# Edge masks in the degree stage, chunk 0 counted before h is split, 33 dense chunks: one change to a graph layer with a mixture of experts

## The chip, the cores and the metric

The kernel runs on one core of a Trainium2 chip. The metric is the time of one execution on the device in microseconds; for the kernel before, three runs gave 1665.93, 1668.72 and 1669.80, median 1668.72. All times inside an execution are read from the trace of one profiled execution, in microseconds from the start of its span. The engines are PE (matrix multiply), DVE (VectorE), ACT (ScalarE), POOL (GpSimd) and SP, which here only issues transfers.

## The reference

A graph of 6250 nodes with 256 features and 200,000 edges (`src`, `dst`, sorted by `dst`). Cut to what matters:

```
deg_out = clip(segment_sum(1, src), 1);  deg_in = clip(segment_sum(1, dst), 1)
h  = x * rsqrt(deg_out)[:, None]
m  = segment_sum(h[src], dst) * rsqrt(deg_in)[:, None]
u  = m @ W_gc + b_gc + (x @ W_res + b_res)
u2 = u + moe(u)           # softmax over the top 2 of 64 experts, 1024 slots each,
                          # expert: gelu(a @ w1 + b1) @ w2 + b2, 256 -> 512 -> 256
out = layernorm(x + batchnorm(u2) * gamma + beta)
```

`batchnorm` takes mean and variance over the nodes, `layernorm` over the features.

## The kernel before, in words

Edges are laid out in groups of 128, one group to a column of the edge tiles: 1563 groups that hold edges, in 1568 columns. Nodes are laid out in 50 tiles of 125.

*Degree stage (L445 to L489).* 49 turns take 32 columns each. In a turn DVE makes two one-hot tiles (`hot_row` and `hot_col`, recorded at L250), PE multiplies them into `degp` (L469), which so counts the out-degree of all nodes, and `project` (L425) multiplies one node tile by W_gc and W_res. The product with W_gc goes to `hrow` and becomes h; because the scaling by the degree is a factor for each row, W_gc is applied before the segment sum. From turn 8 on POOL and PE find, chunk by chunk, how many nodes lie below a place (`ind` L461, `held` L463), and `placed` turns that into offsets. ACT writes `mis` (L490 and the list `off`), the position of each edge's target inside its window of 128 nodes; POOL loads `dstf`, the targets as numbers.

*Seam (L493 to L573).* The degrees are folded into `pd`, clipped, and become `s_out` = 1/sqrt(degree). `dmax`, transposed by PE into `pdm`, tells whether every degree is small enough for an exact count (`okd`, `okc`). DVE computes the edge masks: `kd` is the place of the target inside its short range, `fit` whether it lies within the range the plan allows. The masks end in `key` (chunks), `keyg` (gathered groups), `mf` (the list of edges that fit nowhere, written to DRAM) and `nmis`, from which `redo` and `some` tell a loop at the end whether any edge is left over. Mixed with these lines, `halves(t0)` (L513) scales ten node tiles of h and splits each into two numbers of the matmul's reduced fp32 type, a high half by ACT (L517) and a rest by DVE (L520) or by ACT and POOL (L524, L525), and SP writes both to `h_dram`.

*Dense stage (from L580).* The plan (L76) cuts the edges, which grow sparser with the target's number, into two sorts. The first 1025 groups are 31 *chunks*: for each chunk PE counts, with one-hot tiles `lo` (L250) and `hotk` (L650), how many edges go from every node to every one of the 128 targets of the window (`pc`, L663), ACT adds the counts to the cleared tile `counts[c % 2]` (L674), and 50 multiplies (L681, L682: one for each half of h) turn counts times h into the sums. The counts of chunk c + 1 are issued among the multiplies of chunk c. A `spread` (L698) adds a chunk's sums at their rows. The other 538 groups are *gathered*, in 32 windows: POOL fetches 128 rows of h by an indirect DMA (L596) into a ring of 8 tiles, and PE multiplies by a one-hot of the targets (L601, L602). The code emits all this by hand in one order: the list `work` carries an estimate for each piece, and a gathered group is set in when the estimates add up to `LEAD` plus n times `every`. Steps for finished nodes (x pairs, L715 to L751: two node tiles of u, their logits and top two) run in the same stage; what is not finished by its end, 4 tiles here, is left over to the routing.

*Routing (from L940).* `going` (L973) are tiles of ones with a zero first column, the multiplier of a scan (L1027) that finds each token's rank within its expert; POOL sets them. `upto_b`, `ex` and the picks on DVE come before the scan. Then the experts and the final norms follow.

The order of each engine's instructions is the order in which the code emits them; engines wait for one another only by data and by buffers.

## Time and profile before

| what | us |
|---|---|
| median of three runs (lowest, highest) | 1668.72 (1665.93, 1669.80) |
| profiled execution, its time | 1663.35 |
| its span | 1661.2 |
| last turn of the degree stage ends, degrees read (L494) | 176.3 |
| first count of chunk 0 (L663) | 222.55 |
| first multiply of chunk 0 (L681) | 235.86 |
| first fetch of gathered rows (L596) | 238.06 |
| first and last spread (L698) | 276.2, 998.6 |
| busy: PE, DVE, ACT, POOL (share of the span) | 86%, 57%, 43%, 56% |

Times of day such as 176.3 are starts within the span. A busy PE is not PE at its peak, because matmuls are pipelined: two matmuls in a row may each be shown with 0.28 us though they start 0.12 us apart. The spacing of starts is what they cost. Busy shares over the whole span mix stages with different limits, so windows of one stage are what is to be read.

### The profile page before, as it was taken

To read this page: it belongs to the slowest core of one execution; us is meant where nothing else is said; L and a number is where in the kernel's file an instruction comes from. 1 tells how busy PE (TensorE), PEld (TensorE's weight loads), DVE (VectorE), ACT (ScalarE), POOL (GpSimd) and SP (SyncE) were. 2 spreads that over 40 slices of the span, in tenths; PEclk is the share of its full clock that TensorE was granted. 3 is DMA by queue.
4 is the path that set the end of the run, shared out by engine and by line. 5 is a ranking of instruction groups with operands and counts; after the bars stand their busy time and mean duration, and the time that the engine had idled before them with its cause. 6 is when DMAs were issued, how large, how long until landed. Compare 5 with 4: busy or idle time off the path is not lost. (4 is left out here: it accounts for less than half of the span.)

```text
span 1661.2 us, 30987 instructions
## 1 busy us (share of the span) xinstructions
PE 1430.9 (86%) x10301; PEld 1196.1 (72%) x10301; DVE 940.0 (57%) x1786; ACT 709.9 (43%) x1706; POOL 935.3 (56%) x992
## 2 busy tenths in 40 slices
PE   4999349889999999999999995499999999997920
PEld 2555137778898999999899993378788887875610
DVE  8999876567656566555555537823232232221896
ACT  2343584334565656555555531322222222222258
POOL 3242337777777777777777752056566666652000
PEclk8999759999999999999999996789999999999965
DMA  5899776777887788787878866469788898774924
GB/s 157 230 270 274 239 232 196 202 219 208 237 237 209 219 246 252 209 240 220 230 227 235 232 187 146 131 181 280 218 266 274 258 263 259 222 234 149 250 64 123
DMA packets 221098, 362.14 MB, mean 218 GB/s; under 512 B 24819, under 2 KB 149613, under 8 KB 220929
## 3 DMA queue, kind: packets, MB, share of 16 engines
q1 hardware_dynamic: 158039, 180.12, 37.6%
q0 software_dynamic: 55328, 172.48, 35.5%
q10 hardware_dynamic: 7562, 7.47, 1.6%
q8 instruction: 84, 1.38, 0.3%
q14 instruction: 85, 0.70, 0.1%
HBM read 279.11 MB, written 74.47 MB: 213 GB/s over the span
## 5 line engine op out<-in xcount | busy, mean ns | idle before, releaser
L596 POOL DMA_INDIRECT r<-h_dram,srcg x538 | 579.9, 1078 | 184.4 <-issue 67.4
L681 PE MATMUL sm<-hrow,counts 125*128 125x258 f32 x1550 | 498.8, 338 | 2.6 <-DMA h_dram<-hrow 2.6
L674 ACT CAST counts<-pc 128x300 f32 (+7 forms) x804 | 356.3, 443 | 238.3 <-PE pc L663 203.7
L682 PE MATMUL sm<-hrow,counts 125*128 125x256 f32 x1550 | 412.4, 282 | 0.0
L681 PEld LDWEIGHTS sm<-hrow,counts 125*128 125x128 f32 x1550 | 301.2, 194 | 7.3 <-ACT counts L674 2.8
L650 DVE TENSOR_TENSOR hotk<-key,iota_h 128x1400 bf16<-128x1400 f16 (+5 forms) x199 | 190.3, 958 | 200.0 <-PE pc L663 198.9
L663 PE MATMUL pc<-hotk,lo 128*128 128x300 bf16 (+7 forms) x1025 | 278.3, 306 | 23.9 <-DMA h_dram<-hrow 18.0
L682 PEld LDWEIGHTS sm<-hrow,counts 125*128 125x128 f32 x1550 | 296.1, 191 | 0.9
L1342 ACT ACTIVATE hT<-ph,b1c 128x128 f32<-128x128 f32 (+8 forms) x256 | 112.2, 439 | 331.0 <-PE ph L1340 318.9
L1352 PE MATMUL py<-w2s,hT 128*128 128x256 f32 (+3 forms) x992 | 237.8, 383 | 0.0
L1340 PE MATMUL ph<-xgT,w1s 128*128 128x128 f32 (+8 forms) x1024 | 209.3, 348 | 0.8 <-DVE xgT L1330 0.8
L601 PE MATMUL pg<-r,hot 128*128 128x258 f32 x538 | 177.2, 329 | 25.2 <-DMA r<-h_dram,srcg 24.0
L1352 PEld LDWEIGHTS py<-w2s,hT 128*128 128x128 f32 (+3 forms) x992 | 165.6, 175 | 39.4 <-DVE ys L1355 2.7
L1340 PEld LDWEIGHTS ph<-xgT,w1s 128*128 128x128 f32 x1024 | 169.8, 191 | 33.1 <-issue 13.0
L1306 POOL DMA_INDIRECT y_dram<-ys,dest x124 | 120.2, 969 | 107.8 <-DVE ys L1355 47.3
L1306 POOL DMA_INDIRECT xg<-x_dram,ids x124 | 120.2, 970 | 100.7 <-DVE ids L1257 60.6
L1355 DVE TENSOR_TENSOR ys<-py,b2s 128x256 f32<-128x256 f32 (+3 forms) x124 | 52.3, 422 | 188.6 <-PE py L1352 173.3
L602 PE MATMUL pg<-r,hot 128*128 128x256 f32 x538 | 151.2, 281 | 0.0
L663 PEld LDWEIGHTS <-lo 128*128 128x128 bf16 x1025 | 88.3, 101 | 61.9 <-issue 23.1
L601 PEld LDWEIGHTS pg<-r,hot 128*128 128x128 f32 x538 | 102.8, 191 | 39.6 <-DMA r<-h_dram,srcg 35.6
L832 DVE TENSOR_TENSOR hot<-keyg,iota_f 128x512 fp32r<-128x512 f16 (+3 forms) x146 | 94.4, 648 | 45.7 <-PE pg L602 45.5
L250 DVE TENSOR_TENSOR lo<-lo_b,iota 128x1024 bf16<-128x1024 bf16 x129 | 88.6, 688 | 48.7 <-PE pc L663 48.0
(328 smaller groups left out, 1748.2 us busy)
## 6 DMA issues: line engine op xcount, KB each, us to landing
w1s<-in_L_gnn_w_dram SPq DMA_DIRECT2D x64, 512.0 KB
w2s<-in_L_gnn_w_dram SPq DMA_DIRECT2D x64, 512.0 KB
y_dram<-zeros SPq DMA_DIRECT2D x48, 256.0 KB
yr<-y_dram SPq DMA_DIRECT2D x25, 448.0 KB
r<-h_dram,srcg POOLq DMA_INDIRECT x538, 4.2
b2s<-in_L_gnn_b_dram SPq DMA_DIRECT2D x64, 128.0 KB
h_dram<-hrow SPq DMA_DIRECT2D x5, 1344.0 KB
z_dram<-zeros ACTq DMA_DIRECT2D x7, 903.0 KB
```

The costliest lines, as they stand in the source:

```text
L596: G.indirect_dma_start(out=f32(r[:, :2 * D]), out_offset=None, in_=h_dram[:, :], in_offset=bass.IndirectOffsetOnAxis(ap=idx, axis=0))
L601: T.matmul(pg, hot, r[:, D:], start=first, stop=False)
L602: T.matmul(pg[:, :D], hot, r[:, :D], start=False, stop=last)
L650: V.tensor_tensor(hot, pairs(key, e, n, m), iota_h[:, None, :m, :].to_broadcast([128, n // 2, m, 2]), ALU.is_equal)
L663: T.matmul(pc, los[g // PAIRS][:, r // 2, :, r % 2], hots.pop(g), start=(i == 0), stop=(i == k - 1))
L674: S.copy(counts[c % 2][:, :, ds(live["at"][j % 8], w)], pc.rearrange("p (t w) -> p t w", w=w))
L681: T.matmul(sm, by, hrow[:, t, D:], start=(t == 0), stop=False)
L682: T.matmul(sm[:, :D], by, hrow[:, t, :D], start=False, stop=(t == NT - 1))
L1306: w = G.indirect_dma_start(**kw)
L1340: T.matmul(ph[:, :m], w1s[:, kk, c * 128:(c + 1) * 128], xgT[:, kk, :m], start=(kk == 0), stop=(kk == 1))
L1342: S.activation(hT[:, c, :m], ph[:, :m], AF.Gelu, bias=b1_e[:, c:c + 1])
L1352: T.matmul(py[:n], hT[:, c, k * 128:k * 128 + n], w2s[:, c, :], start=(c == 0), stop=(c == 3))
```

## The change

1. *Masks.* The masks are computed inside the turns of the degree stage, one operation in each of a list of turns (`masks`). `wide` holds the width less one; `kc` is `kd` clamped to the allowed range, `unfit` where that changes it, and the key is `kd` where it fits and far off where not, plus the width times `hi`, which eleven ACT activations make of `wide` in turn 2. `keyg` is written by ACT directly, for gathered groups alone. The sums for `nmis` come out of two ACT passes; `mf` is added and written by POOL in turns 43 and 44. `ind` starts at turn 9 (`FIRST_IND`), `placed` comes two turns later than before with the two added chunks. `away` has a third row, which DVE makes in `placed`.
2. *Seam.* The square root's table is loaded in turn 48; the last two projections come behind the square root and the reciprocal, and `pdm` behind them.
3. *Clears.* Both tiles of counts are cleared at the start: the first in five pieces by DVE, POOL, DVE, POOL, ACT, the second in five by POOL. `counts[1]` is no longer cleared by ACT between the counts of chunk 0.
4. *Halves.* `halves(t)` handles one pair of tiles: two ACT activations and two DVE operations, nothing on POOL. Two pairs stand at the first `hotk` tiles, ten between the counts of chunk 0 (one for every fourth count), thirteen between its multiplies (t = 0, 2, ... 24). The first eight fetches and the first one-hots of gathered rows (`first_rows`) are issued behind the last pair. `left_edges` (the left-over check) stands at t = 45 of chunk 0.
5. *Plan.* 33 chunks with 1061 groups, 502 gathered groups in 30 windows, `LEAD` 76. Six node tiles are left over to the routing.
6. *Routing.* ACT fills `going`.

```diff
-LEAD = 30.0
+LEAD = 76.0
...
-    while 16.0 + 1.03 * (pe + (NGU - g) * 0.265) < (NGU - g) * 1.29:
+    while 16.0 + 1.03 * (pe + (NGU - g) * 0.265) < (NGU - g) * 1.42:
...
+            masks = {
+                8: lambda: V.tensor_tensor(kd, dstf[:, :GD], base, ALU.subtract),
+                11: lambda: V.scalar_tensor_tensor(kc, kd, 0.0, upmost, op0=ALU.max, op1=ALU.min),
+                14: lambda: V.tensor_tensor(unfit, kc, kd, ALU.not_equal),
+                17: lambda: V.scalar_tensor_tensor(kd, unfit, -4096.0, kc, op0=ALU.mult, op1=ALU.add),
+                20: lambda: V.tensor_tensor(key[:, :GD], kd, wide, ALU.add),
+                22: lambda: S.activation(kd, unfit, AF.Copy, accum_out=nmis[:, 0:1]),
+                23: lambda: S.activation(mf[:, :GD], unfit, AF.Copy, scale=-4.0 * FAR, bias=4.0 * FAR),
+                26: lambda: V.tensor_scalar(past, keyg, 0.0, None, op0=ALU.is_ge),
+                29: lambda: V.scalar_tensor_tensor(fit, keyg, float(WIN), past, op0=ALU.is_lt, op1=ALU.mult),
+                30: lambda: S.activation(past, fit, AF.Copy, accum_out=nmis[:, 1:2]),
+                31: lambda: S.activation(mf[:, GD:], fit, AF.Copy, scale=FAR),
+                FIRST_IND + ND + 1: lambda: G.tensor_tensor(mf, mf, dstf, ALU.add),
+                FIRST_IND + ND + 2: lambda: G.dma_start(out=mis_dram, in_=mf),
+            }
...
+                    for g, h, w in wides:
+                        S.activation(wide[:, g:h], hi_b[:, g:h], AF.Copy, scale=float(w))
...
+                if i in masks:
+                    masks[i]()
...
-            project(NT - 1)
...
+            S.activation(s_out, s_out, AF.Sqrt)
             V.scalar_tensor_tensor(dmax, bad[:TP], 2.0 * EXACT, dmax, op0=ALU.mult, op1=ALU.max)
+            V.reciprocal(s_out, s_out)
+            project(NT - 2)
+            project(NT - 1)
             pdm = ps_a.tile([128, TP], F32, name="pdm", tag="pt")
...
-            halves(0)
...
+            counts = [cp.tile([128, NT, WIN], F32R, name=f"counts{i}") for i in range(2)]
+            for i, t0, clear in [(0, t0, c) for t0, c in zip(range(0, NT, 10), (V, G, V, G, None))] +                     [(1, t0, G) for t0 in range(0, NT, 10)]:
...
+            def halves(t):
+                for u in (t - 1, t):
+                    S.activation(hrow[:, u, :D], f32(hrow[:, u, D:2 * D]), AF.Copy, scale=s_out[:, u:u + 1])
+                for u in (t - 1, t):
+                    V.scalar_tensor_tensor(hrow[:, u, D:2 * D], f32(hrow[:, u, D:2 * D]), s_out[:, u:u + 1],
+                                           f32(hrow[:, u, :D]), op0=ALU.mult, op1=ALU.subtract)
...
+                made_of = 1
                 for q in range(KB):
                     hot_of(q)
+                    halves(made_of)
+                    made_of += 2
...
                 for g in range(n):
                     yield of_one_hots(0) / n, lambda g=g: count(g)
+                    if g % 4 == 3:
+                        yield 1.0, lambda t=made_of: halves(t)
+                        made_of += 2
...
+                        if c == 0 and t % 2 == 0 and made_of < NT:
+                            yield 1.0, lambda t=made_of: halves(t)
+                            made_of += 2
+                            if made_of > NT:
+                                yield 0.0, lambda: first_rows()
+                        if c == 0 and t == 45:
+                            yield 0.0, lambda: left_edges()
                         yield 0.24, lambda c=c, t=t: multiply(c, t)
...
-    for g in going:
-        G.memset(g, 1.0)
-        G.memset(g[:, :, 0:1], 0.0)
+    for g, n in zip(going, (NA, NB)):
+        S.activation(g, iota_f[:TP, None, :n].to_broadcast([TP, E, n]), AF.Copy, scale=0.0, bias=1.0)
+        S.activation(g[:, :, 0:1], iota_f[:TP, :E, None], AF.Copy, scale=0.0)
```

More of the change, by code (lines that the diff above doesn't have):

```diff
@@ L510, in gnn_moe_kernel @@
-            V.tensor_scalar(t1, mis, float(WIN), None, op0=ALU.is_lt)
-            V.reciprocal(s_out, s_out)
-            def halves(t0):
-                for t in range(t0 + 1, t0 + 10, 2):
-                    for u in (t - 1, t):
-                        S.activation(hrow[:, u, :D], f32(hrow[:, u, D:2 * D]), AF.Copy, scale=s_out[:, u:u + 1])
-                    for u in (t - 1, t):
-                        if u % 3:
-                            V.scalar_tensor_tensor(hrow[:, u, D:2 * D], f32(hrow[:, u, D:2 * D]), s_out[:, u:u + 1],
-                                                   f32(hrow[:, u, :D]), op0=ALU.mult, op1=ALU.subtract)
-                        else:
-                            whole = ld.tile([TP, D], F32, name="whole")
-                            S.activation(whole, f32(hrow[:, u, D:2 * D]), AF.Copy, scale=s_out[:, u:u + 1])
-                            G.tensor_tensor(hrow[:, u, D:2 * D], whole, f32(hrow[:, u, :D]), ALU.subtract)
-                    if t % 5 == 4 or t % 10 == 5:
-                        n = 6 if t % 10 == 5 else 4
-                        node_dma(nc.sync, False, f32(hrow[:, t + 1 - n:t + 1, :2 * D]), node_rows(h_dram, t + 1 - n, n))
@@ L586, in gnn_moe_kernel @@
                 tc.tile_pool(name="ps_g", bufs=2, space=PSUM) as ps_g:
+            counts = [cp.tile([128, NT, WIN], F32R, name=f"counts{i}") for i in range(2)]
+            for i, t0, clear in [(0, t0, c) for t0, c in zip(range(0, NT, 10), (V, G, V, G, None))] +                     [(1, t0, G) for t0 in range(0, NT, 10)]:
+                piece = counts[i][:, t0:t0 + 10, :]
+                if clear is None:
+                    S.activation(piece, iota_f[:, None, :].to_broadcast([128, 10, WIN]), AF.Copy, scale=0.0)
+                else:
+                    clear.memset(f32(piece), 0.0)
             NR = 8
@@ L855, in gather, with first_rows @@
                     made["gathered"] = i
-            for n in range(NR):
-                fetch(ring[n], srcg[:, rows[n][1] - GD:rows[n][1] - GD + 1])
-            hot_rows(0)
+            def first_rows():
+                for n in range(NR):
+                    fetch(ring[n], srcg[:, rows[n][1] - GD:rows[n][1] - GD + 1])
+                hot_rows(0)
             now, n = 0.0, 0
```

131 lines of the change are left out of this document (57 added, 74 removed).

## The prediction

> **What bounds the kernel now.** I read the busy time by windows first, because the shares over the whole span hide the stages, then the waits, then the order of time at the seams. In the windows the columns are the stretch, its length, busy us (instructions) of PE, PE's weight loads, DVE, ACT and POOL, the granted PE clock, the DMA share and GB/s.
>
> ```profile
> 80.00:120.00 40.00, 40.00 (x509) 23.07 (x508) 38.71 (x27) 16.20 (x52) 17.56 (x13) 1.00 0.91 270
> 187.00:222.50 35.50, 0.37 (x1) 0.08 (x1) 34.50 (x57) 27.49 (x62) 19.52 (x35) 0.50 0.90 282
> 222.50:235.80 13.30, 5.24 (x40) 3.50 (x40) 7.91 (x11) 10.81 (x27) 0.00 (x0) 0.50 0.84 269
> 250.00:300.00 50.00, 43.83 (x337) 36.51 (x336) 31.37 (x47) 22.50 (x68) 38.77 (x36) 1.00 0.70 197
> 600.00:650.00 50.00, 50.00 (x396) 46.98 (x394) 29.77 (x67) 29.54 (x71) 38.59 (x38) 1.00 0.84 241
> ```
>
> The degree stage (to 176) is bound by PE with DVE close behind. From 187 to 222.5 PE stands nearly empty, with 0.37 us of work, while DVE makes the edge masks and, with ACT and POOL, the halves of h. From 250 on PE is the busiest, but not full early on. The seams in order of time (start, length, engine, line, operation; in brackets the idle time before and what ended it):
>
> ```profile
> 176.30 0.26 DVE L494 COPY dsb<-degp 128x100 f32<-128x100 f32 x1 [2.06 <-PE degp L469]
> 187.00 42.93 SPq L166 DMA_DIRECT2D h_dram<-hrow  x20
> 217.90 5.90 ACT L624 ACTIVATE counts<-iota_f 128x1280 fp32r<-128x1280 f32 x5
> 222.55 0.82 PE L663 MATMUL pc<-hotk,lo 128*128 128x100 bf16 x8 [17.96 <-DMA h_dram<-hrow]
> 235.86 0.58 PE L681 MATMUL sm<-hrow,counts 125*128 125x258 f32 x1 [2.59 <-DMA h_dram<-hrow]
> 238.06 1.06 POOL L596 DMA_INDIRECT r<-h_dram,srcg  x1 [18.61 <-issue]
> 252.52 0.36 PE L681 MATMUL sm<-hrow,counts 125*128 125x258 f32 x1
> ```
>
> The degrees are done at 176.3, the first count of chunk 0 starts at 222.55 and the first multiply at 235.86; the last row is the multiply of t = 25, the 26th of chunk 0. The first count is put down to a write of h; it reads `lo` and `hotk` and no h, and what stood last ahead of it on DVE was the masks and the halves. The dense stage is told by the fetches and by the spreads, one for each chunk:
>
> ```profile
> L596 POOL DMA_INDIRECT r<-h_dram,srcg x538 | 579.9, 1078 | 184.4 <-issue 67.4
> L698 PE MATMUL sm<-sums,to x62: 378/381/485, 276.2 to 998.6; 128*128 128x258 f32 x62
> 313.77 0.60 PE L698 MATMUL sm<-sums,to 128*128 128x258 f32 x2
> PE pg L601 <- DMA r<-h_dram,srcg: 24.0, 38, 2.3
> 946.59 0.29 PE L681 MATMUL sm<-hrow,counts 125*128 125x258 f32 x1
> 946.71 0.28 PE L682 MATMUL sm<-hrow,counts 125*128 125x256 f32 x1
> 946.84 0.38 PE L663 MATMUL pc<-hotk,lo 128*128 128x450 bf16 x1
> 946.88 0.46 PE L681 MATMUL sm<-hrow,counts 125*128 125x258 f32 x1
> 947.17 0.28 PE L682 MATMUL sm<-hrow,counts 125*128 125x256 f32 x1
> 947.29 0.28 PE L601 MATMUL pg<-r,hot 128*128 128x258 f32 x1
> ```
>
> POOL is the second limit: (579.9 + 184.4 - 18.6 before the first) / 538 = 1.386 us a fetch, without a pause all stage long. In PE's steady cadence a multiply (two matmuls) costs 0.24, a gathered row the same, a count of 450 columns 947.17 - 946.71 - 0.24 = 0.22. Summed with such spacings over 250 to 998.5 (1529 multiplies 365, 537 gathered rows 130, 927 counts 133, spreads and carries 40, x steps 30) PE has about 697 us of work in 748.5: some 51 us are stalls, by the same sum 34 of them before 450 (the first two spreads are 313.77 - 276.2 = 37.6 apart), where the plan sets 27 to 20 gathered rows in a chunk and POOL cannot deliver faster.
>
> **The change, part by part.** Masks moved into the degree turns.
>
> ```profile
> 154.08 1.21 DVE L250 TENSOR_TENSOR hot_row<-row_b,iota 128x2048 bf16<-128x2048 bf16 x1
> 156.95 1.21 DVE L250 TENSOR_TENSOR hot_row<-row_b,iota 128x2048 bf16<-128x2048 bf16 x1
> 172.32 0.95 PE L469 MATMUL degp<-hot_col,hot_row 128*64 128x100 bf16 x32
> 175.32 0.87 PE L469 MATMUL degp<-hot_col,hot_row 128*64 128x100 bf16 x29
> 176.48 1.22 DVE L501 TENSOR_TENSOR key<-dstf,base 128x1025 f16<-128x1025 f32 x1
> ```
>
> A turn costs PE 3.00 and DVE 2.87. Seven DVE operations enter turns 8 to 29: five over 1061 columns at up to 1.22, two over 507 at about 0.3 to 0.6, 6 to 7 us in all. Over 22 turns the slack is 22 × 0.13 = 2.9, plus DVE's lead of about 2 us over PE: 5 of 6.5 are covered, so +1.4 (0 if the slack is a little larger, +6.5 if none is left). On ACT the turns gain four passes and eleven small rescalings of `wide` and lose 31 writes of the mask; ACT is busy 16.2 of 40 in these turns, so nothing. POOL's `ind` chain starts a turn later and ends with the mask's add and its DMA at turn 44, where POOL is idle half the time: nothing; without that cover its add would cost its 3.48 us (below).
>
> The path from the degrees to the first count.
>
> ```profile
> 178.38 1.94 PE L425 MATMUL pr<-wcat,fT 128*125 128x512 f32 x4
> 180.16 0.27 PE L507 MATMUL pdm<-ident,dmax 125*128 125x125 f32 x1
> 180.97 1.28 ACT L508 ACT_TABLE_LOAD   x1
> L250 DVE TENSOR_TENSOR lo<-lo_b,iota 128x1024 bf16<-128x1024 bf16 x8 | 5.4, 687 | 7.2 <-PE pc L663 7.2
> L650 DVE TENSOR_TENSOR hotk<-key,iota_h 128x1800 bf16<-128x1800 f16 x5 | 5.3, 1090 | 1.2 <-PE pc L663 1.2
> L624 ACT ACTIVATE counts<-iota_f 128x1280 fp32r<-128x1280 f32 x10 | 12.3, 1264 | 0.0
> L550 DVE TENSOR_SCALAR okc<-okc,okd 128x31 f32<-128x31 f32 x1 | 3.2, 3233 | 0.0
> L544 POOL TENSOR_TENSOR mf<-mf,dstf 128x1568 f32<-128x1568 f32 x1 | 3.5, 3482 | 0.1
> 1004.15 2.55 POOL L974 MEMSET going<- 125x2944 bf16 x1
> 1004.19 2.84 DVE L967 TENSOR_SCALAR upto_b<-iota_f,pidx 128x128 bf16<-128x128 f32 x1
> ```
>
> After `dsb` (177.7 with the 1.4) come `pd` 0.5, two projections 4.0 and `pdm` 0.3, so that pdm lands at about 182; the table load no longer stands in the chain. Behind pdm on DVE stand `okd` and `okc` (0.7), two clears of `counts` (priced by the ACT row, 1.26 each, 2.5), `lo` 0.68 and `hotk` 1.09: first count at about 187. The seven POOL clears start at the same moment as `okc`. The rows show what that can do: `okc`, over 31 columns, took 3.23 while POOL's L544 ran 3.48, and L967, over 128 columns, took 2.84 beside a POOL memset of 2.55. So between 0.7 and 7 us are added (one clear to most of the seven); I take 3, as POOL's clears come as separate instructions between which DVE can enter. First count 190, against 222.55: 32 us earlier. The Trainium skill, "SBUF — State Buffer", section "SBUF: two separate sides", says that the port pair of DVE and GpSimd is a lock held for a whole instruction by whichever came first; the two pairs of rows agree. By it DVE loses at most one clear for each of its own operations, some 4 us, against my 3.
>
> Counts of chunk 0, with ten pairs of halves in between.
>
> ```profile
> L517 ACT ACTIVATE hrow<-hrow,s_out 125x256 fp32r<-125x256 f32 x50 | 21.6, 493 | 0.5 <-DVE s_out L511 0.5
> L520 DVE SCALAR_TENSOR_TENSOR hrow<-hrow,s_out 125x256 fp32r<-125x256 f32 x33 | 18.1, 604 | 2.4 <-ACT hrow L517 2.4
> L674 ACT CAST counts<-pc 128x100 f32 x20 | 5.2, 261 | 2.5 <-issue 1.4 <-ACT counts L624 0.6
> ```
>
> For four counts and a pair of halves ACT needs 2 × 0.29 + 2 × 0.43 = 1.45 and DVE 2 × 0.48 to 2 × 0.60 + 0.34 (`lo`) + 0.24 (`hotk`) = 1.5 to 1.8; ten of them are 15 to 20 (13.3 before, which held five clears instead). First multiply at about 208 (203 to 213), 28 earlier. Half of the gain is then given back: turns t = 0 to 24 of chunk 0 hold 13 more pairs. DVE and ACT need 1.5 to 1.9 us for each beside the counts of chunk 1; with waits between them I take 2.4 (2.0 to 2.7), 31 us for the 25 turns, so t = 25 stands at about 239 (229 to 248). Before, it stood at 252.52. Net at this point: 13.5 us earlier (4 to 23). What sets the first fetch is unchanged: it needs all of h written, and that write is 12.8 MB, at the 280 GB/s of the windows 46 us. It began at 187 and can begin at about 190 now, so the fetch comes at 238 to 244 against 238.06, and nothing is gained there. But the plan now asks for the first gathered row only in chunk 1 (about 249), when eight rows are there.
>
> The dense stage. Two chunks more and 36 groups counted instead of gathered: 2 × (50 × 0.24 + 0.87 for the spread) + 36 counts × 0.215 = 33.5; less 36 gathered rows × 0.242 = 8.7 and two windows' carries 0.9: +24 us of PE work; one x pair fewer in the stage gives 1.3 back, and the seven little operations of the left-over check with a PE transpose at t = 45 cost 0.7. From t = 25 at 252.52 on, the 697 of before are 695; so 695 + 24 - 1 = 718 us. Of the 51 us of stalls I expect 15 left (8 to 20): the plan puts 23, 23, 20, 20, 19 rows in chunks 1 to 5 where it put 27, 25, 22, 22, 20, and 15 instead of 16.5 in the late ones. 23 × 1.386 = 32 us of fetching in a chunk that holds about 32 of PE work, 15 × 1.386 = 21 in one of 22. POOL's 502 × 1.386 = 696 from 243 ends at 939, ahead of PE. So PE ends the stage at 239 + 718 + 15 = 972 against 998.6: **-26.5** (-10 to -40).
>
> Routing. Four left-over tiles become six: one more x pair and two more tiles of top-two, about +3.2 on DVE. In exchange `going` is set by ACT, and `upto_b` should fall from 2.84 to some 0.2, -2.6. Net +0.6 (-1 to +3). The experts and the end are untouched.
>
> Sum: -26.5 + 0.6 = -26 on an execution of 1663.35 (span 1661.2), so 1637.5 for one like it. That execution lies 5.4 below the median of 1668.72 (and 2.6 below the lowest of the three runs), so on the median's scale I say **1643**, for this likeliest case 1630 to 1658.
>
> **The rivals.**
> Slower, the dense stage is really PE's: the waits give PE only 24.0 us behind fetched rows, and if the other 27 are PE's own (a slower cadence where counts, gathers and spreads mix) they stay with the chunks, and so does the rest, since the fetches stay near their limit. Then the stage has +23 of work, keeps 45 of stalls (-6) and starts 13.5 earlier: +3.5, with routing +4: 1673. It is slower as soon as more than 41 us of stalls stay (15 + 26). Against it: the window 600:650 shows the same mix on PE with no stall to see.
> Less gain, the seam is slower: the POOL clears hold DVE for 7, and the halves keep ACT and DVE at 2.6 a pair. t = 25 comes at 250 and the first rows with it, 11 later: 1654.
> Less gain, the masks are not hidden: DVE paces turns 8 to 30 and all the 6.5 us land ahead of the degrees: 1648.
> More gain: with rows always ready the stalls fall to 8 and t = 25 comes at 234: 1631.
>
> **How the numbers follow.** Forecast 0.56, slower rival 0.15, slow seam 0.14, masks 0.07, more gain 0.08. The range, 1629 to 1667, leaves out most of the slower rival and the tail of the best. A difference under 0.2% (3.3 us) can't be told from none: 1665.4 to 1672.1. All cases but the slower rival give faster, less a tail of the slow seam: faster 0.80, same 0.06, slower 0.14.
>
> **What would show it.** `dsb` at 176 to 179; the first count near 190 and the first multiply near 208; no stretch longer than 8 us without PE work between 180 and 240; the first fetch at 238 to 244; early spreads 32 to 34 us apart instead of 37.6, late ones still about 22; the last spread at 972; PE's wait for rows under 8 us; `upto_b` at 0.2. Wrong it would be if t = 25 of chunk 0 comes after 250, if the spreads of chunks 2 to 6 stand as far apart as before, or if late chunks grow beyond 22.4 us.

## The result, and the profile after

The changed kernel is faster, by less than forecast: median 1654.27 us (1651.05 to 1656.41, 7 runs) against 1668.72 us (1661.87 to 1670.41, 7 runs), ratio 0.993 with a 95% interval of 0.991 to 0.9951. The forecast was 1643 with a range of 1629 to 1667; the time lies in the range and on the forecast side, but the gain is about half of what was said: 12 us by the ratio and 14 by the medians, instead of 26. The profiled execution took 1651.05 us (span 1649.2), 12.0 less than that of before in span.

First the rows in order of time that answer to those of before (start, length, engine, line, operation; in brackets the idle time before and what ended it):

```profile
185.97 0.26 DVE L528 COPY dsb<-degp 128x100 f32<-128x100 f32 x1 [3.05 <-PE degp L500]
190.71 7.84 POOL L563 MEMSET counts<- 128x1280 f32 x7 [25.37 <-DMA y_dram<-zeros]
191.14 0.77 DVE L544 TENSOR_SCALAR okc<-okc,okd 128x33 f32<-128x33 f32 x1
196.05 0.82 PE L659 MATMUL pc<-hotk,lo 128*128 128x100 bf16 x8 [5.46 <-issue]
199.85 41.88 SPq L166 DMA_DIRECT2D h_dram<-hrow  x20
210.92 0.58 PE L675 MATMUL sm<-hrow,counts 125*128 125x258 f32 x1 [3.12 <-ACT counts L670]
237.34 0.56 PE L675 MATMUL sm<-hrow,counts 125*128 125x258 f32 x1
247.34 1.07 POOL L574 DMA_INDIRECT r<-h_dram,srcg  x1 [48.25 <-issue]
990.32 0.19 DVE L976 TENSOR_SCALAR upto_b<-iota_f,pidx 128x128 bf16<-128x128 f32 x1
```

The degrees are done 9.7 us later than before. From there to the first count it takes 10.1 us instead of 46.3. The multiply of t = 25 stands at 237.34, 15.2 earlier than before, and the first fetch at 247.34, 9.3 later. `upto_b` is down to 0.19, as forecast. The dense stage by its spreads, by windows (stretch, its length, busy us and instructions of PE, PE's weight loads, DVE, ACT, POOL, granted PE clock, DMA share, GB/s) and by PE's wait for rows:

```profile
L692 PE MATMUL sm<-sums,to x66: 378/381/485, 259.6 to 984.2; 128*128 128x258 f32 x66
237.30:254.90 17.60, 15.17 (x100) 13.37 (x98) 12.77 (x28) 8.37 (x27) 6.04 (x6) 0.69 0.63 193
400.00:950.00 550.00, 550.00 (x4265) 518.10 (x4263) 317.08 (x659) 322.38 (x718) 408.76 (x382) 1.00 0.78 221
PE pg L579 <- DMA r<-h_dram,srcg: 6.5, 14, 1.4
```

From 400 to 950 PE's row has no idle time left: behind the first chunks it is the bound, and its wait for fetched rows fell from 24.0 to 6.5 us. The last spread starts at 984.2 instead of 998.6: 14.4 us gained there, of which the routing gives 1.7 back (first expert matmul 87.8 us behind the last spread instead of 86.0), and the experts and the final norms together 0.8.

By the terms of the forecast (us, profiled executions):

| stretch | forecast | measured |
|---|---|---|
| degrees done, later than before | +1.4 | +9.7 |
| degrees done to t = 25 of chunk 0 | 61.3 | 51.4 |
| t = 25 to the last spread | 733 | 746.9 |
| last spread to the end, longer than before | +0.6 | +2.5 |

### The profile page after: what moved, and what is told of

Same layout as the page of the kernel before. It is cut to its first block, busy times and chain, and to the rows that moved or that the text cites. A ratio compares the mean times of both kernels' runs of the same rounds, so it can differ in the third digit from the quotient of the medians.

```text
span 1649.2 us, 31317 instructions
## 1 busy us (share of the span) xinstructions
PE 1459.2 (88%) x10475; PEld 1223.9 (74%) x10475; DVE 943.4 (57%) x1800; ACT 713.1 (43%) x1710; POOL 928.7 (56%) x941
## 3 DMA queue, kind: packets, MB, share of 16 engines
q1 hardware_dynamic: 157760, 179.87, 37.5%
## 5 line engine op out<-in xcount | busy, mean ns | idle before, releaser
L574 POOL DMA_INDIRECT r<-h_dram,srcg x502 | 539.4, 1075 | 229.4 <-issue 81.8
L675 PE MATMUL sm<-hrow,counts 125*128 125x258 f32 x1650 | 530.9, 339 | 3.1 <-ACT counts L670 3.1
L670 ACT CAST counts<-pc 128x300 f32 (+7 forms) x840 | 376.0, 448 | 226.4 <-PE pc L659 185.8
L676 PE MATMUL sm<-hrow,counts 125*128 125x256 f32 x1650 | 439.3, 283 | 0.0
L675 PEld LDWEIGHTS sm<-hrow,counts 125*128 125x128 f32 x1650 | 322.6, 196 | 9.5 <-ACT counts L670 3.3
L646 DVE TENSOR_TENSOR hotk<-key,iota_h 128x1800 bf16<-128x1800 f16 (+5 forms) x209 | 201.8, 967 | 204.8 <-PE pc L659 203.7
L676 PEld LDWEIGHTS sm<-hrow,counts 125*128 125x128 f32 x1650 | 317.1, 192 | 1.1
L659 PE MATMUL pc<-hotk,lo 128*128 128x300 bf16 (+7 forms) x1061 | 293.5, 312 | 22.2 <-DVE lo L250 7.6
L579 PE MATMUL pg<-r,hot 128*128 128x258 f32 x502 | 165.3, 329 | 6.6 <-DMA r<-h_dram,srcg 6.5
L1339 DVE COPY xgT<-pte 128x256 f32<-128x256 f32 (+7 forms) x64 | 38.5, 602 | 129.2 <-PE pte L1337 129.1
L492 POOL TENSOR_SCALAR ind<-iota_f,pos 128x128 bf16<-128x128 f32 x33 | 80.2, 2433 | 49.4 <-PE held L494 47.7
```

The lines of the kernel that those rows point to most:

```text
L574: G.indirect_dma_start(out=f32(r[:, :2 * D]), out_offset=None, in_=h_dram[:, :], in_offset=bass.IndirectOffsetOnAxis(ap=idx, axis=0))
L579: T.matmul(pg, hot, r[:, D:], start=first, stop=False)
L646: V.tensor_tensor(hot, pairs(key, e, n, m), iota_h[:, None, :m, :].to_broadcast([128, n // 2, m, 2]), ALU.is_equal)
L659: T.matmul(pc, los[g // PAIRS][:, r // 2, :, r % 2], hots.pop(g), start=(i == 0), stop=(i == k - 1))
L670: S.copy(counts[c % 2][:, :, ds(live["at"][j % 8], w)], pc.rearrange("p (t w) -> p t w", w=w))
L675: T.matmul(sm, by, hrow[:, t, D:], start=(t == 0), stop=False)
```

## The experiments

They ran in five groups, each on a chip of its own: e1 to e4; c1 with e5 to e7; c2 with f1 and f3; g1; and h1 to h4. In the first three groups the kernel before took 1760 to 1776 us, in the other two 1665 to 1666, as in the first runs. No chip ran two groups, so a difference of chips and one of times of day can't be told apart; the text speaks of slower chips for short. Times are compared within a group, or as ratios to the kernel before in the same group. A turn is counted from 0 and lasts from the turn before it to its own first multiply of `degp`; turns of single traces differ at the start of the stage by up to 3 us, so stretches of it are compared from turn 6 or 41 on where that matters.

**Two masks alone (g1).** The kernel before with two DVE operations added and nothing else.

```diff
+                if i == 8:
+                    V.tensor_tensor(key[:, :GD], dstf[:, :GD], base, ALU.subtract)
+                if i == 11:
+                    V.scalar_tensor_tensor(key[:, :GD], key[:, :GD], 0.0, upmost, op0=ALU.max, op1=ALU.min)
                 if i >= 8:
```

> The kernel before with nothing changed but two DVE operations of 1025 columns (1.2 us each) in turns 8 and 11; what they write is overwritten later. Theory (lock): 2.5 us of DVE work, but DVE then has no gap for some ten turns, one ind on POOL takes 8 to 16 us instead of 1.35, and one or two turns between 10 and 17 take 5 to 7 us: the degrees are done 4 to 6 us later than in the kernel before (180 to 182 instead of 176.3). Rival (DVE time): what is not covered by DVE's lead of two turns is paid, 0 to 1 us, no turn is over 4 us, and no ind over 3 us.

Turns 11 and 12 took 6.77 and 5.47 us instead of 3.06, every other turn behind them 3.0 to 3.2 as before, and the degrees were done at 181.82 instead of 176.30. The time went from 1664.56 to 1668.73 (ratio 1.0024, 1.0006 to 1.0042). Rows of this kernel in order of time:

```profile
55.67 10.26 POOL L465 TENSOR_SCALAR ind<-iota_f,pos 128x128 bf16<-128x128 f32 x3 [23.41 <-PE held L467]
64.83 0.19 PE L467 MATMUL held<-ones_b,ind 128*128 128x1 bf16 x1 [3.24 <-POOL ind L465]
67.10 1.23 DVE L250 TENSOR_TENSOR hot_row<-row_b,iota 128x2048 bf16<-128x2048 bf16 x1 [2.79 <-PE degp L473]
74.01 1.35 POOL L465 TENSOR_SCALAR ind<-iota_f,pos 128x128 bf16<-128x128 f32 x1 [2.45 <-PE held L467]
```

An `ind` takes 0.60 us when DVE is idle and 1.35 in the steady turns, where DVE has a gap of 0.1 us in each. With the two masks DVE runs without a gap from turn 8 on, and the first `ind` is stuck from 55.67 to 64.78, while DVE goes from one operation to the next. PE waits for it (3.24), so DVE runs out of free one-hot tiles and waits for PE (2.79), and there POOL gets in: the `ind` ends 0.47 us behind the last DVE operation ahead of that wait. The rival, by which no `ind` takes over 3 us, falls. The changed kernel shows the same picture:

```profile
58.92 10.26 POOL L492 TENSOR_SCALAR ind<-iota_f,pos 128x128 bf16<-128x128 f32 x3 [26.18 <-PE held L494]
65.75 1.81 DVE L250 TENSOR_TENSOR hot_col<-col_b,iota 128x3200 bf16<-128x3200 bf16 x1
68.09 0.19 PE L494 MATMUL held<-ones_b,ind 128*128 128x1 bf16 x1 [3.26 <-POOL ind L492]
70.32 1.23 DVE L250 TENSOR_TENSOR hot_row<-row_b,iota 128x2048 bf16<-128x2048 bf16 x1 [2.75 <-PE degp L500]
86.56 2.35 POOL L492 TENSOR_SCALAR ind<-iota_f,pos 128x128 bf16<-128x128 f32 x1 [0.62 <-PE held L494]
88.45 1.30 DVE L250 TENSOR_TENSOR hot_row<-row_b,iota 128x2048 bf16<-128x2048 bf16 x1
159.62 4.82 POOL L459 TENSOR_TENSOR mf<-mf,dstf 128x1568 f32<-128x1568 f32 x1
161.01 3.48 DVE L411 TENSOR_TENSOR away<-pos,rows_w 128x33 f32<-128x33 f32 x1
164.85 0.27 PE L414 MATMUL pp<-ident,away 128*33 128x128 f32 x1 [1.99 <-DVE away L412]
```

Its turns 12 and 13 took 6.75 and 5.62: 6.2 us over 3.06, less what the turns before them gained, makes the 5.8 by which it stands behind the kernel before from turn 13 on. The first of the three `ind` was stuck for 9.11 us, to 0.47 behind the end of the `hot_col` that starts at 65.75. The last three rows are a second knot, at turns 42 and 43 (5.26 and 4.70): `mf` takes 4.82 instead of its 3.48, and `away`, an operation of 0.18, stands until `mf` is done.

The fifth and sixth row show that POOL doesn't always have to wait for a stop of DVE. From turn 18 on DVE's row in the changed kernel has no gaps either, yet each `ind` ended after 2.2 to 3.3 us, 0.46 us behind the start of a DVE operation that took 0.08 longer than elsewhere (1.30 for a `hot_row`, 1.90 for a `hot_col`), and the turns stayed at 3.06. What lets POOL in between two DVE operations there, and not around turn 12, the traces don't show.

**held later (e1).** Each `ind` gets three turns instead of one.

```diff
-                        at_or_past[c] = dp.tile([128, 128], BF16, name="ind", bufs=2)
+                        at_or_past[c] = dp.tile([128, 128], BF16, name="ind", bufs=4)
...
-                    if 1 <= c <= ND:
-                        T.matmul(held[:, c - 1:c], at_or_past[c - 1], ones_b[:, :1], start=True, stop=True)
-                    if c == ND:
+                    if 3 <= c < ND + 3:
+                        T.matmul(held[:, c - 3:c - 2], at_or_past[c - 3], ones_b[:, :1], start=True, stop=True)
+                    if c == ND + 2:
                         placed()
```

> The changed kernel, with the matmul that reads each ind tile (held) three turns behind the ind instead of one, and four ind tiles instead of two; past takes the place of kc to make room. Theory (POOL): in the changed kernel turns 12 and 13 take 6.75 and 5.62 us because DVE, with a mask in every third turn, has no gap, POOL's ind cannot get at SBUF between DVE's operations, and PE waits for held. Then a later held gives POOL three turns, turns 12 and 13 go back to about 3.06, and the degrees are done 4 to 6 us earlier (180 to 182 instead of 185.97); the time falls by about as much. Rival (DVE): the masks' own DVE time, 5.9 us, is what is lost; then the turns stay long wherever DVE runs out and the degrees stay at 185 to 186. At turns 42 and 43, where mf on POOL stands against away on DVE, 1.5 to 4 us are still lost.

Half a miss. Turns 12 and 13 were 3.04 and 3.05, but turns 16 and 17 took 7.95 and 4.25, 6.1 us over 3.06 where the changed kernel lost 6.2: this loss was put off, not avoided. The degrees were done at 185.71. From turn 6 to there it took 137.0 us, against 139.0 in the changed kernel and 129.1 in the kernel before; most of those 2 us are won behind turn 41.

```profile
66.63 18.74 POOL L492 TENSOR_SCALAR ind<-iota_f,pos 128x128 bf16<-128x128 f32 x5 [28.68 <-PE held L494]
```

The first of these five was stuck for 16.4 us, through a dozen DVE operations, until DVE had to wait again (it ended 0.47 us behind the last of them). So time to spare at the reader did not help.

**mf later (e2).**

```diff
-                31: lambda: S.activation(mf[:, GD:], fit, AF.Copy, scale=FAR),
-                FIRST_IND + ND + 1: lambda: G.tensor_tensor(mf, mf, dstf, ALU.add),
-                FIRST_IND + ND + 2: lambda: G.dma_start(out=mis_dram, in_=mf),
+                46: lambda: S.activation(mf[:, GD:], fit, AF.Copy, scale=FAR),
+                47: lambda: G.tensor_tensor(mf, mf, dstf, ALU.add),
+                48: lambda: G.dma_start(out=mis_dram, in_=mf),
```

> The changed kernel, with the last ACT pass over mf in turn 46, its add on POOL in turn 47 and its DMA in turn 48. Theory: turns 42 and 43 of the changed kernel (5.26 and 4.70 instead of 3.0) are long because away (DVE, 33 columns, 3.48 us) waits until mf's add on POOL is done; with the add after placed, away takes 0.2, both turns 3.0 to 3.1, and the degrees are done 3 to 4 us earlier, at 182 to 183; the add itself may hold one DVE operation of turn 48 or the seam, 0 to 2 us. Rival: placed itself is late because held is; then nothing changes there.

As the theory said: `away` took 0.18, turns 42 and 43 were 3.14 and 3.19, and from turn 41 to the degrees it took 3.6 us less than in the changed kernel. (They were done at 183.82, since this execution was already 1.4 us later at turn 11.)

The times of the e1 group don't tell these runs from the changed kernel: as ratios to the kernel before 0.976 (0.972 to 0.98) for held later and 0.9754 (0.9713 to 0.9796) for mf later, against 0.9752 for the changed kernel in the two other slow groups. What they show is in the turns.

**ind on ACT (e5, and once more h1)**, with the later `mf`.

```diff
-                        G.tensor_scalar(at_or_past[c], iota_f, pos[:, c:c + 1], None, op0=ALU.is_ge)
+                        S.activation(at_or_past[c], iota_f, AF.Relu, bias=neg[:, c:c + 1])
+                        S.activation(at_or_past[c], at_or_past[c], AF.Relu, scale=-1.0, bias=ones[:, :1])
```

(`neg` holds one less the place; `placed` adds `held` instead of subtracting it.)

> The changed kernel with ind made by two ACT operations instead of one on POOL (it then marks the places below, and the sign of held is turned), and mf's add in turn 47. Theory (lock): with nothing on POOL that PE waits for, DVE may run without a gap; turns 12 and 13 and turns 16 and 17 stay at 3.0 to 3.1, turns 42 and 43 too, and the degrees are done 8 to 10 us earlier than in the changed kernel, at 176 to 178. The masks' own DVE time then costs 0 to 2 us. Rival (DVE time): the 5.9 us of masks are paid wherever DVE has to make them; then DVE sets the pace of a run of turns from 11 to 30 (each some 3.1 to 3.3) and the degrees are done at 181 to 183. The time falls by 8 to 10 us against the changed kernel on this chip, or by 3.5 to 4.5.

> ind on ACT and the later mf, as before in another group, as the measure for the three that follow. Where the fetches run at 1.39 to 1.44 us a row: 7 us below the changed kernel, ratio to before 0.989.

In the h1 group the degrees were done at 176.85 instead of 185.97, turns 12, 13, 42 and 43 at 3.05, 3.06, 3.14 and 3.19; in the c1 group at 178.38 against 185.12 for the changed kernel on the same chip. From turn 6 to the degrees h1 took 130.23 us, against 129.08 in the kernel before. So the same DVE masks cost next to nothing once POOL is out of the way, and the rival (DVE's time) falls. Turn 16 stays long (3.93 and 4.51), in the c1 group turn 22 too (3.88): ACT, which now makes `ind` behind `hx`, waits in turn 16 for a transfer of `hrow`.

```profile
PE held L496 <- ACT ind L494: 0.7, 1, 0.7
176.85 0.26 DVE L530 COPY dsb<-degp 128x100 f32<-128x100 f32 x1 [1.60 <-PE degp L502]
L694 PE MATMUL sm<-sums,to x66: 378/380/485, 251.6 to 983.6; 128*128 128x258 f32 x66
```

The time is 1648.56, ratio 0.9898 (0.9857 to 0.994), that is about 5 us below the changed kernel by the ratios, with intervals that overlap; 1724.96 against 1732.02 in the c1 group, there too with intervals that overlap. The degree stage gave 9 us, but the last spread stands at 983.6, only 0.6 before that of the changed kernel. What took the rest lies in the first chunks: from the first spread to the sixth it took 149.8 us instead of 142.5, and the first hundred fetches went at 1.45 us each instead of 1.39. The rows below are the 107th fetch, the last that PE uses ahead of the sixth spread, and that spread, first in the changed kernel, then with `ind` on ACT:

```profile
394.31 1.48 POOL L574 DMA_INDIRECT r<-h_dram,srcg  x1 [0.30 <-PE pc L659]
402.06 0.60 PE L692 MATMUL sm<-sums,to 128*128 128x258 f32 x2
393.73 1.44 POOL L576 DMA_INDIRECT r<-h_dram,srcg  x1 [0.30 <-PE pc L661]
401.43 0.60 PE L694 MATMUL sm<-sums,to 128*128 128x258 f32 x2
```

In both the spread stands 7.7 us behind that fetch. The multiply of t = 25 came 8.4 us earlier and the first fetch 7.1, but the 107th fetch only 0.6: the fetches set the pace of these chunks, and PE gave the early start back in stalls (35.5 us from t = 25 to the last spread by the prices of the forecast, 27.8 in the changed kernel). The idle time ahead of each of the first hundred fetches was alike (0.31 us), the fetches themselves took 1.15 us instead of 1.09. These are single executions, and why the fetches were slower there is not settled.

**More multiplies in chunk 0**, alone (e3) and with `ind` on ACT (e7); their result is not used.

```diff
+                if c == 0 and t < 40:
+                    T.matmul(banks[1][:, :D], by, hrow[:, t, :D], start=True, stop=True)
```

> The changed kernel with one matmul more behind each multiply of t = 0 to 39 of chunk 0, into a bank of PSUM that nothing uses then; its result is not used. Theory: from 211 to 248 PE runs at half clock for want of work, and from t = 25 to the end of chunk 0 it is PE at half clock that sets the pace (17.6 us where the cadence at full clock gives about 10). If the extra work brings the full clock by t = 25, chunk 0 ends 3 to 6 us earlier in spite of 40 matmuls more. Rival: DVE and ACT set the pace there; then the end of chunk 0 does not move, or moves back by the extra matmuls, 5 to 8 us.

> The kernel with ind on ACT and the later mf, with the additional multiplies of t = 0 to 39 of chunk 0 as well. In their own run these multiplies brought the full clock 8 us sooner: from the first multiply to the end of chunk 0 it was 41.3 us instead of 44.0 in the changed kernel. Theory (half clock costs time there): 2 to 3 us earlier at the end of chunk 0 than without them, and up to as much off the time, if the first fetch, which does not move, does not take it back. Rival: PE waits for fetched rows then, and the time is the same within 1 us.

The clock came up: the row below is the window of e3 from t = 25 to the end of chunk 0, at clock 1.00 where the changed kernel had 0.69 for the same stretch.

```profile
232.90:249.50 16.60, 12.64 (x115) 11.39 (x113) 12.96 (x28) 8.41 (x28) 2.38 (x2) 1.00 0.53 164
```

But the stretch took 16.6 us at full clock and 17.6 at 0.69. From the first multiply to the end of chunk 0 it took 41.3 with the added multiplies and 44.0 in the changed kernel, and with `ind` on ACT 42.8 and 43.7. By these single traces the half clock costs some 1 to 3 us, not 6. PE, DVE and ACT are each idle for a part of this stretch; it holds 46 counts of chunk 1 with 25 copies and 12 one-hot tiles, in turns, and before the change it took as long (16.66). The times with `ind` on ACT, 1728.37 with the added multiplies and 1724.96 without, do not differ; alone, the added multiplies gave a ratio of 0.9784 (0.9738 to 0.983), no better than the changed kernel's 0.9752.

**Three pairs of halves first**, alone (e4), and then with LEAD 62, `ind` on ACT and the later `mf` (f1 and h3).

```diff
             V.reciprocal(s_out, s_out)
+            for t in range(1, 6, 2):
+                halves(t)
             project(NT - 2)
```

> The changed kernel with three pairs of halves right behind the reciprocal, ahead of the last two projections, the clears and the one-hots; ten pairs then remain for the multiplies of chunk 0. Theory: the first fetch (247.34) waits for the write of h, which starts at 199.85 and runs at the full 280 GB/s of the transfers; begun at 192 to 194 it ends 5 to 7 us earlier, first fetch at 240 to 242, and PE's stalls at the start of the stage shrink: 2 to 6 us off the time. The first count comes 1 to 2 us later. Rival: gathers are not what PE waits for between 237 and 260 (half clock, counts); then the fetch moves and the time stays within 2 us.

> ind on ACT and mf's add in turn 47, three pairs of halves right behind the reciprocal, LEAD 62 instead of 76 (the first gathered group in t = 34 of chunk 0 instead of chunk 1), and the three small DVE operations of the left-over check at t = 34, away from its PE transpose at t = 45. In the run with the halves first POOL fetched eight rows from 243.6 on, then stood still for 9.9 us with its ring full until the first gathered group at 263.3, and PE stood 5.7 us behind the left-over check. Theory: where fetches set the pace (1.55 us a row), what counts is when they start and that they never stop: first fetch at 236 to 238, first gathered group 3 to 5 us behind it, and the stage ends 10 to 16 us earlier than in the changed kernel; time 12 to 18 us below it. Where PE sets the pace (1.44), 8 to 12 us below it. Rival: PE, not the fetches, sets the end in both; then only the 7 us of the degree stage are seen.

> ind on ACT, later mf, three pairs of halves first, LEAD 62. If the early stalls (6 us in the second half of chunk 0, 15 us from 250 to 350) come from the late start of the fetches, they shrink to 8 to 12 in all and it is 8 to 12 us faster than with ind on ACT alone. Rival: PE's work and the counts of chunk 1 set chunk 0's end; then it is the same within 4 us.

Alone it was the slowest of its group, 1723.11 against 1715 to 1717. The first fetch came at 243.6, 58.1 us behind the degrees instead of 61.4. The write of h does set it, but by its end and not by its start: it began 9.0 us earlier than in the changed kernel (190.84), while the last of its twenty pieces, behind the last halves, was issued 4.2 earlier (236.83 against 241.04), and the fetch followed 6.8 and 6.3 us behind that. The first gathered group came at 263.3 (256.7 in the first trace of the changed kernel), and POOL stood still:

```profile
POOL r L587 <- PE pg L593: 9.9, 1, 9.9
PE sm L619 <- DVE nmis L617: 5.7, 1, 5.7
```

With LEAD 62 the first gathered group came 4.2 us behind the first fetch, as meant. In the c2 group that gave 1723.50 against 1734.49 for the changed kernel (ratios 0.9695, 0.9675 to 0.9715, and 0.9752, 0.973 to 0.9774): 11 us, just under the 12 to 18 expected, of which `ind` on ACT alone had given 7 in the c1 group. In the h1 group it gave nothing beyond `ind` on ACT: 1648.65 against 1648.56. The first fetch there was 4.8 us earlier, at 235.4, but chunk 0 ended 4.8 us later, since gathered groups now stand among its multiplies, and up to the sixth spread PE took 114 fetched groups instead of 107. The last spread stands at 981.8, only 1.8 earlier. There the rival holds.

**How many chunks.** The changed kernel with the plan's 31 chunks, and the kernel of the last group with 35; the changed kernel itself twice as their measure.

```diff
-    while 16.0 + 1.03 * (pe + (NGU - g) * 0.265) < (NGU - g) * 1.42:
+    while 16.0 + 1.03 * (pe + (NGU - g) * 0.265) < (NGU - g) * 1.29:
```

(1.55 for 35 chunks, with 1095 groups counted and 468 gathered. In order: the changed kernel c1; 31 chunks e6 and h2; the changed kernel c2; 35 chunks f3 and h4.)

> The changed kernel itself, once more, to have its times and its trace on the same chip as the others of this group: turns 12, 13, 42 and 43 of the degree stage long again (6.7, 5.6, 5.3, 4.7), and a time against the kernel before that tells whether the gain depends on the pace of the fetches, which was 1.55 us a row in the four runs ahead of this and 1.44 in the first trace. If the pace is 1.44 here, the ratio to before is about 0.993; if it is 1.55, the ratio should be some 0.98, since 36 fewer fetches save more than the two chunks cost.

> The changed kernel with the plan of before: 31 chunks, 538 gathered groups. It tells what the two chunks are worth behind the new seam. By the sum of the prediction PE has 24 us less to do, but POOL has 36 fetches more: at 1.39 to 1.44 us they end 50 to 52 us later than in the changed kernel, at about 1017 to 1020, and PE some 12 us behind them: 20 to 40 us slower than the changed kernel. Rival (PE is the bound): without the two chunks it is up to 20 us faster.

> The changed kernel with 31 chunks. Theory (fetches bound): first fetch at about 247, 538 of them at 1.387 us end at 993, PE some 15 us behind them at 1005 to 1010, against 984 with 33 chunks and 998.6 in the kernel before: 20 us slower than the changed kernel, and up to 10 slower than before. Rival (PE bound): PE has 24 us less work and ends at 965 to 975, 10 to 20 us faster than the changed kernel.

> The changed kernel a third time, as the measure for the two that follow on the same chip. Ratio to before 0.993 if the fetches run at 1.39 to 1.44 us a row here, about 0.975 if at 1.55.

> The same with 35 chunks (1095 groups counted, 468 gathered). At 1.55 us a row 34 fewer fetches save 53 us of POOL's time against 23 us more work of PE, whose work is then about 740 us from t = 25: the two balance, and the stage ends 15 to 30 us earlier than with 33 chunks. At 1.44 us PE is the bound already and it ends 15 to 23 us later.

> The same with 35 chunks. With fetches at 1.39 to 1.44 PE is the bound from 350 on already with 33 (no stall in the trace of the changed kernel), so the 25 us more of work are paid in the late chunks and 8 to 12 us of early stalls are saved: 10 to 18 us slower than with 33. With pauses at the fetches it is some 25 us faster, as in the group before.

| ratio to the kernel before | kernel before 1665 to 1669 us | kernel before 1775 to 1776 us |
|---|---|---|
| new seam, 31 chunks | 0.9976 (0.9953 to 0.9999) | 1.0001 (0.9975 to 1.0026) |
| the changed kernel, 33 | 0.993 (0.991 to 0.9951) | 0.9752 (both groups) |
| better seam, 33 (h3, f1) | 0.9909 (0.9874 to 0.9945) | 0.9695 (0.9675 to 0.9715) |
| better seam, 35 (h4, f3) | 0.9997 (0.9972 to 1.0022) | 0.9576 (0.955 to 0.9603) |

The new seam alone, with 31 chunks, is worth 4 us on the one kind of chip and nothing on the other: the fetches start no earlier and there are as many of them, so POOL ends them when it did. Rows of the 31-chunk kernel of the h1 group:

```profile
L574 POOL DMA_INDIRECT r<-h_dram,srcg x538 | 574.3, 1067 | 216.1 <-issue 97.8
PE pg L579 <- DMA r<-h_dram,srcg: 31.4, 39, 2.3
```

538 fetches from 251.63 to 989.23 are 1.37 us each, with PE waiting 31.4 us for them. With two chunks more PE works more and waits 6.5. So the rival that PE is the bound before the change falls: taking the two chunks away makes it slower by 8 us (0.9976 against 0.993; 20 were expected) and by 42 (1774.19 against 1732.02), not faster by up to 20. At 35 chunks the kinds of chip part: 15 to 18 us slower on the one, where PE was full with 33 already, 26 faster on the other. The first row is the changed kernel's of the c1 group, the second that of 35 chunks on such a chip:

```profile
400.00:950.00 550.00, 518.51 (x3944) 481.85 (x3942) 294.47 (x611) 293.39 (x672) 386.87 (x349) 1.00 0.72 203
400.00:950.00 550.00, 547.77 (x4219) 514.61 (x4218) 308.59 (x636) 324.24 (x723) 364.92 (x336) 1.00 0.71 198
```

With 33 chunks PE has 31 us without work there, and none in the first trace (550.00 of 550). What happens on the slower chips is seen in the fetches of the changed kernel (c1 group):

```profile
599.91 0.95 POOL L574 DMA_INDIRECT r<-h_dram,srcg  x1 [0.30 <-issue]
601.17 1.31 POOL L574 DMA_INDIRECT r<-h_dram,srcg  x1 [0.30 <-PE sm L676]
602.79 0.95 POOL L574 DMA_INDIRECT r<-h_dram,srcg  x1 [0.30 <-PE sm L676]
604.96 0.95 POOL L574 DMA_INDIRECT r<-h_dram,srcg  x1 [1.23 <-PE pc L659]
```

Most fetches take 0.95 us as elsewhere, with 0.30 ahead of them, but about every sixth has some 1.2 ahead of it; with 31 chunks that makes 1.55 us a fetch between 400 and 900, against 1.38 in the kernel before on the first chip. What POOL waits for in those pauses the traces don't tell.

## Why the prediction was half right

Right in kind: the sign, the place of the gain, and what bounds the late chunks. The stretch between the degrees and the first count is down from 46.3 us to 10.1; two chunks more trade 24 us of PE's work (719 us from t = 25 by the prices of the forecast, 718 said) for fetches; and from 400 to 950 PE stalls for 2.9 us by the same prices.

The gain was half of what was said, and the terms tell where it went: the masks cost 8.3 us more than forecast, the seam 9.9 less, t = 25 to the last spread 13.9 more, the end 1.9 more. That masks and seam cancel is luck. Two steps failed: the masks' step in its mechanism, and the step that left 15 us of stalls in its size; the second is what the time lacks.

*The masks failed in the mechanism.* "POOL's `ind` chain ... nothing" and "POOL is idle half the time: nothing" were wrong. DVE's own time for the masks was sized well (with `ind` on ACT the degrees are done 0.6 us later than before in the one trace, and 1.2 when counted from turn 6; +1.4 was forecast). What was left out is that an operation on POOL, idle or not, can be kept from SBUF by a run of DVE operations, here of six and of twelve. POOL's slack was counted, and the gap in DVE's row, 0.1 us a turn, was not seen as what POOL used. The trace of before has a sign of it:

```profile
102.17 1.35 POOL L461 TENSOR_SCALAR ind<-iota_f,pos 128x128 bf16<-128x128 f32 x1 [1.71 <-PE held L463]
```

Turns 9 to 38 of that trace, with an `ind` each, took 3.06 us, and an `ind` 1.35 instead of 0.60; the 3.00 of the forecast was read behind 154, where no `ind` runs any more. The loss was 5.8 us at turns 12 and 13 and 3.9 at turns 42 and 43, 9.7 against 1.4; the second part the forecast had named, as the 3.48 of `mf` without its cover. (`placed` stands in turn 42, three turns later than before and not two.) The lock had been used in the forecast, but at the seam, where it turned out to cost about 0.6 us: `okc` took 0.77 and ended with the first POOL clear (191.91 and 191.88), and the DVE clears took 1.12 each beside seven POOL clears. The Trainium skill, "SBUF — State Buffer", section "SBUF: two separate sides", has the distinction: DVE operations with two SBUF inputs contend only with POOL operations that read SBUF. The forecast's bound of some 4 us left it out. The traces agree: `ind` and `mf` read and were stuck (9.1, 16.4 us) or held DVE up (3.48 us for an operation of 0.18); the clears read nothing. That one operation is passed over by six or twelve of the other engine's is shown by these runs alone. That the rival "masks not hidden" had 6.5 us at 0.07 was the right place with the wrong mechanism.

*The seam was priced 10 too dear.* First count 10.1 us behind the degrees (12.3 forecast), first multiply 14.9 behind that (18), t = 25 26.4 behind that (31). With the degrees 9.7 late, t = 25 came at 237.34 instead of 239: two errors that cancel.

*The stalls were priced 13 too cheap: this is the step that the time shows.* 28 us by the same sum instead of 15 (8 to 20): 6.5 between t = 25 and 250, 15.0 up to 400, 6.3 behind. Two parts of the term were wrong. One is the second half of chunk 0, 17.6 us for 9.4 of PE's work by the prices of the sum, with the counts of chunk 1 in it; the half clock in it was measured at 1 to 3 us. The other is the balance of the early chunks. The forecast set 32 us of fetching against a chunk that "holds about 32 of PE work". By its own prices, with the counts priced by their columns, the stretches from the first spread to the fourth hold 26 us of PE's work each, with 24, 23 and 20 rows to fetch, which is 33, 32 and 28 us at 1.386. They took 29.1, 33.4 and 28.4 us, 12 us of stalls in all: there the fetches still set the pace, and from the fourth stretch on PE's work is as long as the fetching. In the kernel before the same stretches held 27 to 28 us of work in 37.5, 35.0 and 32.3, so the trace that the forecast was made from could tell it.

The first fetch came at 247.34, 61.4 us behind the degrees, where 238 to 244 was forecast from a write that could "begin at about 190"; it began at 199.85, and the fetch followed 47.5 us behind, where 46 was said. How much of the stalls this lateness made is open: in h3 the first fetch was 4.8 us earlier than in h1, but its plan also put 7 more fetched groups ahead of the sixth spread, and the time was the same. The early chunks, with 105 fetched rows in five, stay bound by fetches; there a change of 4% in the pace is 6 us.

*Routing*: `upto_b` fell as forecast, but the stretch grew by 1.7 instead of 0.6; not followed up.

The fastest kernel measured on a chip like the first is the changed one with `ind` on ACT and the later `mf`, 1648.56 us (0.9898), with h3 (1648.65) not to be told from it; on the slower ones the one with 35 chunks, 1697.45 against 1734.49 for the changed kernel.

## What to carry to other kernels

Before work is packed into an engine's last gaps, ask who else uses those gaps: an operation on POOL that reads SBUF may be passed over while DVE runs back to back, and if the main chain reads its result, 2.5 us of DVE work cost 5.5 here. Price a moved operation by what it keeps others from as well as by its own time, and rather let nothing on POOL feed PE in a stage that DVE fills. Price the two limits of a stage chunk by chunk: one pace for the whole stage hid that the first chunks hold 26 us of PE's work and up to 33 of fetches. When two limits lie within a few per cent (here 15 fetches at 1.39 and 22 us of PE's work a chunk), the plan's best point moves with the chip, so measure it on more than one.

## What the runs showed of the hardware that was not expected

- One POOL operation of 0.60 us took 9.1 us (changed kernel, and the kernel before with two masks) and 16.4 us (held later): six and twelve DVE operations went ahead of it, and it ended 0.47 us behind the last one ahead of a wait of DVE. In the steady turns of the kernel before it took 1.35, with a gap of 0.1 us in DVE's row; in the later turns of the changed kernel 2.2 to 3.3, with no gap and one DVE operation a turn 0.08 longer.
- The same kernel before took 1665 to 1669 us in some groups and 1760 to 1776 in others, each group on its own chip. Traces of the changed kernel and of its variants show pauses of about 1.2 us at every sixth indirect fetch in the slower groups; the degree stage ran alike, turn by turn 3.06 us.
- The same change is worth 0.7% on one chip and 2.5% on another, as fetches or PE's work set the pace there.
